# A four-layer conv kernel: layer 3 of the last image written out by hand in halves of its positions

## The chip, the cores and the metric

The kernel runs on one core of a Trainium2 chip. The metric is device time in microseconds for one launch. The kernel before took 2767.3 us (median of three runs, 2765.76 to 2767.45).

## What is computed

Two images of 512 channels and 32x32 positions go through four layers in f32: a deformable attention block with an MLP (layer 0), a global self-attention (layer 1), a position attention (layer 2) and a non-local block with squeeze-and-excitation (layer 3). The change touches the end: the results of layer 2 and all of layer 3, for the second image. Layer 3 is, per image:

```python
x_avg = jnp.mean(x, axis=(2, 3), keepdims=True)
se_mid = jax.nn.relu(conv1x1(x_avg, se1_w, se1_b))
W_cw = jax.nn.sigmoid(conv1x1(se_mid, se2_w, se2_b))
g_x = conv1x1(x, g_w, g_b).reshape(b, N)
theta_x = conv1x1(x, theta_w, theta_b).reshape(b, N)
phi_x = conv1x1(x, phi_w, phi_b).reshape(b, N)
f = theta_x[:, :, None] * phi_x[:, None, :]
f_div_C = jax.nn.softmax(f, axis=-1)
y = jnp.einsum('bij,bj->bi', f_div_C, g_x)
W_y = conv1x1(y, W_w, W_b)            # y has one channel
...
return W_cw * W_y + x                  # W_y after a batch norm with given statistics
```

So theta, phi and g are one number per position. For each of 1024 positions a softmax over 1024 others is taken of theta times phi, and g is averaged with it. The result y, one number per position, is scaled and shifted per channel and added to x.

## The kernel before

The image lies with channels on partitions: x2 is 128 x 4 x 2048 (four blocks of channels, two images of 1024 positions). Layers 0 and 1 come first and fill most of the time. Then image 0 goes through layer 2; after it, image 0's layer 3 is interleaved with image 1's layer 2 (`part(t)` is called between image 1's `l2_h` and `l2_attn` steps), and image 1's layer 3 comes last with nothing to interleave.

The functions that matter here:

- `l2_attn` (line 1416): 8 blocks of 128 positions of layer 2's attention. It exponentiates scores straight from PSUM (line 1435).
- `l2_out` (line 1445): z for both halves of 512 positions (`pz`, line 1450, eight accumulated matmuls each; copied by ScalarE, line 1457), then for each half and each block of channels a matmul `pr` (line 1461) and a VectorE instruction that adds it to x in place and sums x for the average (line 1469). `pr` has two PSUM buffers.
- `l3_scores` (line 1473): the rows theta, phi and g by four matmuls per half with 32 output partitions each (`prow`, line 1482), one two-bank PSUM tile for both halves, copied to SBUF (`rows3`, line 1489, ScalarE for half 0 and VectorE for half 1). A matmul with a broadcast selector spreads phi and then g over all partitions (`pp3`, line 1497), ScalarE copies each half to SBUF with its bias (`pg`, line 1504), VectorE takes the maximum and minimum of phi (lines 1508 and 1509). Transposes (line 1513) bring theta to one column per block of 128 positions (`th`, lines 1514 and 1517). `nm` (lines 1520 to 1524) is what is subtracted in the exponent.
- `part(t)` (line 1528): for one block of 128 positions ScalarE computes the exponential of 128x1024 with its sum (line 1530) and VectorE multiplies by g and sums (line 1538). `nd` collects numerators and denominators; `e3` has three buffers.
- `l3_out` (line 1544): y for all eight blocks (lines 1546, 1547), the squeeze-and-excitation weights `cw` (lines 1551 to 1568), `aff` with a scale and a shift per channel (line 1570), y broadcast to all partitions by eight matmuls (`py`, line 1575), and four results of 128x1024: block 0 by VectorE then ScalarE (1586, 1587), the others by ScalarE then VectorE (1589, 1590), each stored by the SP queue (1591), 512 KB each.

Order: outside of layer 0's hand-made part, a scheduler of the framework places the instructions on each engine; an instruction wrapped in `tc.keep_in_program_order` keeps its place in the order of the source on its engine. Each engine works its queue in order. Of this end, GpSimd (POOL) does nothing before the change: its last instruction is a memset of layer 1 (line 1289). The SP queue issues the stores.

## Time and profile before

| what | before |
|---|---|
| median of 3 runs | 2767.3 us |
| the profiled execution's own time | 2764.49 us |
| its span | 2762.7 us |
| TensorE busy | 2707.0 us (98%) |
| VectorE, ScalarE, GpSimd busy | 82%, 56%, 24% |
| granted TensorE clock, mean of the span | 0.996 |
| from the end of image 1's z matmuls to the end | 2718.25 to 2762.7 us |
| in 2735 to 2763 us: PE, DVE, ACT busy | 5.28, 15.66, 15.00 us of 28.00 |
| stores at the end (4 of 512 KB): issue to landing | 2.8 us (median) |

The profile is of one execution. PE is TensorE, DVE VectorE, ACT ScalarE, POOL GpSimd, SP the queue that issues the stores. L1538 is line 1538 of the kernel before. A group's line gives engine, operation, tiles written and read, shapes, count, then busy time and the mean of one, then idle time of the engine ahead of it and who ended it. The chain of waits is followed back from the last instruction; its lines are start, length and what ran. "issue" in it is time in which the profile shows no work and no wait. Matmuls in f32 appear as two passes, so one of 128x512 counts twice.

### The profile page before, as it was taken

The numbers are of one execution on the slowest core, as the hardware profiler recorded it, in microseconds if no ns is written. First come the engines' busy times: TensorE is split into PE (matmuls) and PEld (weight loads), VectorE is DVE, ScalarE is ACT, GpSimd is POOL, SyncE is SP. The second block draws the span as 40 slices with busy tenths as digits, with TensorE's granted clock in tenths as the row PEclk, the third lists the DMA queues.
The fourth block names the chain that finished last, engine by engine and source line by source line (L and its number), as shares of the span: only waits on it lengthen the run. The fifth ranks groups of instructions, "written<-read, shape, count | busy, mean of one in ns | idle before, by whom it ended". The sixth has DMA issues, their size and how long they took to land.

```text
span 2762.7 us, 49727 instructions
## 1 busy us (share of the span) xinstructions
PE 2707.0 (98%) x19782; PEld 987.5 (36%) x19782; DVE 2266.7 (82%) x2473; ACT 1544.3 (56%) x1950; POOL 663.6 (24%) x776
## 2 busy tenths in 40 slices
PE   8999999999999999999999999999999999999996
PEld 4233323233332323333333333333344444455543
DVE  6999999999999999999999999999654545523555
ACT  6676677667667776766776676676321111001244
POOL 0333333333333333333333333333100000000000
PEclk9999999999999999999999999999999999999998
DMA  3777777777777777777787778777400000100001
GB/s 121 160 163 155 161 154 160 158 160 158 154 164 149 162 163 158 161 161 156 167 185 172 152 165 193 154 170 159 102 30 23 16 23 23 70 7 0 0 1 61
DMA packets 145479, 335.14 MB, mean 121 GB/s; under 512 B 22592, under 2 KB 32064, under 8 KB 144480
## 3 DMA queue, kind: packets, MB, share of 16 engines
q0 software_dynamic: 77824, 201.38, 41.1%
q1 hardware_dynamic: 66992, 130.08, 13.2%
q8 instruction: 156, 2.56, 0.4%
q14 instruction: 75, 0.61, 0.1%
q10 hardware_dynamic: 432, 0.51, 0.1%
HBM read 58.99 MB, written 4.46 MB: 23 GB/s over the span
## 4 chain that ended last, share of the span: by engine, by line
PE 93%; ACT 3%; DVE 2%; issue 1%; DMA 1%; ACTq 0%; DVEq 0%; POOL 0%; SPq 0%; POOLq 0%
PE ph L616 61%; PE A L1101 4%; PE D L1101 4%; PE C L1101 4%; PE psim L669 2%; PE pr L1348 2%; PE B L1101 2%; PE po L1036 2%; PE pg L1244 1%; PE psim L654 1%; PE pz L1450 1%; PE pa L1339 1%; PE pu L1278 1%; ACT r L625 1%; PE pscore L1421 1%
## 5 line engine op out<-in xcount | busy, mean ns | idle before, releaser
L616 PE MATMUL ph<-h,w2a 128*32 128x512 f32 x16384 | 1790.7, 593 | 7.0 <-ACT r L625 6.9
L625 ACT ACTIVATE r<-ph,sb 128x1024 f32<-128x1024 f32 x1024 | 1141.4, 1115 | 562.3 <-PE ph L616 541.1
L349 DVE CUSTOM_DVE_ANT_1 h<-tab 128x1024 f32<-128x1024 f32 x1024 | 1205.9, 1220 | 8.6 <-PE ph L616 4.7
L616 PEld LDWEIGHTS ph<-h,w2a 128*32 128x32 f32 x16384 | 533.5, 109 | 1217.5 <-issue 833.1
L631 DVE SCALAR_TENSOR_TENSOR r<-r,rel,r 128x1024 f32<-128x1024 f32 x512 | 656.0, 1281 | 28.0 <-ACT r L625 27.3
L646 POOL DMA_DIRECT2D xs<-r x512 | 476.9, 1144 | 196.0 <-PE ph L616 95.7
L634 POOL DMA_DIRECT2D r<-r x256 | 222.2, 868 | 1107.2 <-DVE r L631 931.1
L172 ACT ACTIVATE tab<-tab,vec 128x256 f32<-128x256 f32 x252 | 137.1, 544 | 0.0
L1289 POOL MEMSET M<- 128x512 f32 x2 | 1.0, 520 | 439.6 <-DVE x L1165 439.6
L1141 ACT COPY u<-A 128x512 f32<-128x512 f32 x16 | 9.4, 585 | 146.9 <-PE A L1101 146.9
L1120 ACT ACTIVATE h<-h,vec 128x512 f32<-128x512 f32 x32 | 23.1, 721 | 113.6 <-DVE h L1123 113.6
L669 PE MATMUL psim<-xs,cw 128*32 128x512 f32 x512 | 72.1, 592 | 2.1 <-DMA xs<-r 2.1
L1123 DVE TENSOR_TENSOR h<-C,u 128x512 f32<-128x512 f32 x32 | 22.1, 691 | 48.8 <-PE C L1101 48.5
L1101 PE MATMUL A<-xn,w 128*128 128x512 f32 x128 | 60.2, 593 | 0.8 <-DVE x L1043 0.8
L1101 PE MATMUL C<-hT,w 128*128 128x512 f32 x128 | 60.3, 592 | 0.0
L1101 PE MATMUL A<-h,w 128*128 128x512 f32 x128 | 60.1, 592 | 0.0
L1036 PE MATMUL po<-q,vwo 128*128 128x512 f32 x128 | 56.4, 594 | 0.0
L1348 PE MATMUL pr<-x,A 128*128 128x512 f32 x128 | 55.1, 592 | 0.0
L229 DVE SCALAR_TENSOR_TENSOR acc<-q,vec,acc 128x128 f32<-128x128 f32 (+3 forms) x88 | 46.2, 525 | 0.8
L1161 DVE TENSOR_TENSOR x<-D,x 128x512 f32<-128x512 f32 x32 | 22.1, 691 | 26.0 <-PE D L1101 26.0
L852 ACT ACTIVATE e<-e,den 128x64 f32<-128x64 f32 x128 | 41.7, 336 | 2.7 <-DVE den L848 2.7
L1161 DVE TENSOR_TENSOR x<-C,x 128x512 f32<-128x512 f32 x32 | 22.1, 690 | 24.8 <-PE C L1101 24.8
(288 smaller groups left out, 1770.3 us busy)
## 6 DMA issues: line engine op xcount, KB each, us to landing
r<-r POOLq DMA_DIRECT2D x256, 512.0 KB, 4.7
xs<-r SPq DMA_DIRECT2D x512, 128.0 KB, 2.4
xs<-r POOLq DMA_DIRECT2D x512, 128.0 KB, 4.8
tab<-fd SPq DMA_DIRECT2D x63, 512.0 KB, 6.0
lw<-in_l_w_dram SPq DMA_DIRECT2D x5, 1024.0 KB, 10.2
x<-in_x_dram SPq DMA_DIRECT2D x4, 1024.0 KB, 8.5
w<-in_mlp_w_dram SPq DMA_DIRECT2D x8, 512.0 KB, 4.2
w<-in_mlp_w_dram SPq DMA_DIRECT2D x16, 256.0 KB, 3.2
```

The costliest lines, as they stand in the source:

```text
L172: return nc.scalar.activation(tf, tf if src is None else src[:, :, :, ax, :], AF.Identity, bias=0.0 if ax == 0 else v("L0_conv_cpb_b1"), s ...
L229: pin(nc.vector.scalar_tensor_tensor(dst, src, wt_, dst, ALU.mult, ALU.add))
L349: nc.vector._custom_dve(TENSOR_ADD_SAT, out=h1[:, h], in0=tab[:, j, h, 0, :].unsqueeze(1).to_broadcast([P, 32, 32]), in1=tab[:, j, h, 1, : ...
L616: nc.tensor.matmul(ph[t * 32 : (t + 1) * 32, i, :], lhsT=w2a[:, o], rhs=h1s[2 * p + i][:, h, half * 512 : (half + 1) * 512], start=True, s ...
L625: pin(nc.scalar.activation(r, ph, AF.Relu, bias=sb3[:, o, 1:2]))
L631: pin(nc.vector.scalar_tensor_tensor(r0, r1, rel[:, i : i + 1], r0, ALU.mult, ALU.add))
L634: pin(nc.gpsimd.dma_start(rs[p, 0], rs.pop((p, 2)), accum_op=ALU.add))
L646: pin(nc.gpsimd.dma_start(rs[p][i::2], r[i::2, i, :], accum_op=ALU.add))
L669: nc.tensor.matmul(psims[g, kb][m * 32 : (m + 1) * 32, :], lhsT=cw3[:, 3 - i : 35 - i], rhs=rs.pop(p + m), start=False, stop=(i == 3), ski ...
L1036: nc.tensor.matmul(po, lhsT=vwo[:, k * B + t // 2, o * P : (o + 1) * P], rhs=q[:, k, ts_], start=(k == 0), stop=(k == KC - 1),)
L1101: nc.tensor.matmul(banks[bank], lhsT=a[an][k], rhs=b_[bn_][k], start=(i < 4 and k == 0), stop=(k == n - 1), skip_group_check=True,)
L1348: nc.tensor.matmul(pr, lhsT=A[b][:, k, o * P : (o + 1) * P], rhs=x[:, k, ns], start=(k == 0), stop=(k == KC - 1),)
```

## The change

The second image's layer 2 results and layer 3 move into one new function, `last`, in which every instruction is wrapped in `keep_in_program_order`. In it:

- the work is cut into two halves of 512 positions; rows of half 0 are computed between results of layer 2, those of half 1 after them; each half has its own one-bank PSUM tile;
- theta's, phi's and g's biases are added when the rows are copied to SBUF (`b3`), phi and g stay in PSUM (two tiles of two banks from layer 2's score pool), the exponentials and the weighted sums read them there, the four copies to SBUF (`pg`) are gone;
- the squeeze-and-excitation weights are computed between the first weighted sums;
- y is formed and broadcast by halves, after the fourth and after the eighth weighted sum; results of the first half stand between the later weighted sums;
- results are 128x512: for blocks 0 to 2, POOL first adds the shift to x in place (`raised`), and VectorE then scales y and adds (`final`); for block 3, ScalarE scales and shifts y and POOL adds x (`final_act`);
- eight stores of 256 KB take the place of four of 512 KB, in the order of the source on the SP queue.

The built program has, besides, a library reload on POOL ahead of its first addition, and waits by which ScalarE's and VectorE's reads of one tile of y follow each other in the source's order (`final_act(3, 0)` after `final(1, 0)`, `final(2, 0)` after `final_act(3, 0)`, `final(0, 1)` after `final_act(3, 1)`).

```diff
@@ -1590,6 +1590,208 @@
                 nc.vector.tensor_tensor(r, r, xs, ALU.add)
             nc.sync.dma_start(out[b, o * P : (o + 1) * P].rearrange("c h w -> c (h w)"), r)
 
+    def last(b, fp, gp, fps, ps, gps, at2, ht):
+        pin = tc.keep_in_program_order
+        ve, pe, act = nc.vector, nc.tensor, nc.scalar
+        b3 = gp.tile([P, 1], F32, name="b3")
+        for i, name in enumerate(("theta", "phi", "g")):
+            first_ = i == 0
+            pin(
+                ve.tensor_tensor(b3, ident[:, i : i + 1], v(f"L3_conv_{name}_b"), ALU.mult)
+                if first_
+                else ve.scalar_tensor_tensor(b3, ident[:, i : i + 1], v(f"L3_conv_{name}_b"), b3, ALU.mult, ALU.add)
+            )
+        z = fp.tile([P, HW], F32, name="z")
+        rows3 = gp.tile([P, 2, 512], F32, name="rows3")
+        th = gp.tile([P, 8], F32, name="th")
+        ext = gp.tile([P, 2, 2], F32, name="ext")
+        top = gp.tile([P, 2], F32, name="top")
+        nm = gp.tile([P, 2, 8], F32, name="nm3")
+        nd = gp.tile([P, 2, 8], F32, name="nd")
+        y = gp.tile([P, 8], F32, name="y")
+        prow, pt = {}, {}
+        def at(o, half):
+            return x[:, o, b * HW + half * 512 : b * HW + (half + 1) * 512]
+        def out_z(half):
+            pz = ps.tile([P, 512], F32, name="pz", tag="ps")
+            for t in range(8):
+                rhs = at2[:, t, half * 512 : (half + 1) * 512]
+                pin(pe.matmul(pz, lhsT=ht[:, t, :], rhs=rhs, start=(t == 0), stop=(t == 7)))
+            pin(act.copy(z[:, half * 512 : (half + 1) * 512], pz))
+        def out_x(half, o):
+            pr = ps.tile([P, 512], F32, name="pr2", tag="ps")
+            zs = z[:, half * 512 : (half + 1) * 512]
+            pin(pe.matmul(pr, lhsT=l2wv[:, o * P : (o + 1) * P], rhs=zs, start=True, stop=True))
+            xs = at(o, half)
+            pin(
+                ve.scalar_tensor_tensor(
+                    xs, pr, v("L2_conv_bv", o), xs, ALU.add, ALU.add, accum_out=xavg[:, o, b, half : half + 1]
+                )
+            )
+        def row(half, k):
+            if k == 0:
+                prow[half] = gps.tile([P, 512], F32, name=f"prow{half}", tag="l3")
+            pin(
+                pe.matmul(
+                    prow[half][k * 32 : (k + 1) * 32, :], lhsT=w3x[:, k, :], rhs=at(k, half), start=True, stop=True
+                )
+            )
+            if k == KC - 1:
+                pin(act.activation(rows3[:, half, :], prow[half], AF.Identity, bias=b3))
+        pp = [fps.tile([P, 2, 512], F32, name="pscore") for _ in range(2)]
+        def spread(half, i):
+            to_all = c("sel3")[:, i : i + 1].to_broadcast([P, P])
+            pin(pe.matmul(pp[i][:, half, :], lhsT=to_all, rhs=rows3[:, half, :], start=True, stop=True))
+        def turn(half):
+            pt[half] = gps.tile([P, 4, P], F32, name=f"ptl{half}", tag="l3")
+            for t in range(4):
+                pin(pe.transpose(pt[half][:, t, :], rows3[:, half, t * P : (t + 1) * P], ident))
+        def theta(half):
+            rows_ = pt[half].rearrange("p t (k r) -> p t k r", k=KC)[:, :, :, 0]
+            pin(ve.tensor_reduce(th[:, half * 4 : half * 4 + 4], rows_, AX.X, ALU.add))
+        def extremes(half):
+            pin(ve.tensor_reduce(ext[:, 0, half : half + 1], pp[0][:, half, :], AX.X, ALU.max))
+            pin(ve.tensor_reduce(ext[:, 1, half : half + 1], pp[0][:, half, :], AX.X, ALU.min, negate=True))
+        def exponential(t):
+            e3 = es[t] = gp.tile([P, HW], F32, name="e3", bufs=3)
+            pin(
+                act.activation(
+                    e3,
+                    pp[0].rearrange("p a n -> p (a n)"),
+                    AF.Exp,
+                    bias=nm[:, 0, t : t + 1],
+                    scale=th[:, t : t + 1],
+                    accum_out=nd[:, 1, t : t + 1],
+                )
+            )
+        def weighted(t):
+            e3 = es.pop(t)
+            g3 = pp[1].rearrange("p a n -> p (a n)")
+            pin(ve.scalar_tensor_tensor(e3, e3, 1.0, g3, ALU.mult, ALU.mult, accum_out=nd[:, 0, t : t + 1]))
+        def mean(half):
+            hs = slice(half * 4, half * 4 + 4)
+            pin(ve.reciprocal(y[:, hs], nd[:, 1, hs]))
+            pin(ve.tensor_tensor(y[:, hs], y[:, hs], nd[:, 0, hs], ALU.mult))
+            py[half] = ps.tile([P, 512], F32, name="pyl", tag="ps")
+            for t in range(4):
+                to_all = y[:, half * 4 + t : half * 4 + t + 1].to_broadcast([P, P])
+                pin(pe.matmul(py[half][:, t * P : (t + 1) * P], lhsT=to_all, rhs=ident, start=True, stop=True))
+        def store(o, half, r):
+            pin(
+                nc.sync.dma_start(
+                    out[b, o * P : (o + 1) * P].rearrange("c h w -> c (h w)")[:, half * 512 : (half + 1) * 512], r
+                )
+            )
+        def raised(o, half):
+            xs = at(o, half)
+            pin(nc.gpsimd.tensor_tensor(xs, xs, aff[:, 1, o : o + 1].to_broadcast([P, 512]), ALU.add))
+        def final(o, half):
+            r = gp.tile([P, 512], F32, name="rl", bufs=6)
+            pin(ve.scalar_tensor_tensor(r, py[half], aff[:, 0, o : o + 1], at(o, half), ALU.mult, ALU.add))
+            store(o, half, r)
+        def final_act(o, half):
+            r = gp.tile([P, 512], F32, name="rl", bufs=6)
+            pin(act.activation(r, py[half], AF.Identity, bias=aff[:, 1, o : o + 1], scale=aff[:, 0, o : o + 1]))
+            pin(nc.gpsimd.tensor_tensor(r, r, at(o, half), ALU.add))
+            store(o, half, r)
+        es, py = {}, {}
+        out_z(0)
+        out_z(1)
+        for o in range(KC):
+            out_x(0, o)
+        out_x(1, 0)
+        out_x(1, 1)
+        for k in range(KC):
+            row(0, k)
+        out_x(1, 2)
+        out_x(1, 3)
+        for i in range(2):
+            spread(0, i)
+        for k in range(KC):
+            row(1, k)
+        turn(0)
+        extremes(0)
+        theta(0)
+        spread(1, 0)
+        turn(1)
+        spread(1, 1)
+        extremes(1)
+        theta(1)
+        pin(ve.tensor_reduce(top, ext, AX.X, ALU.max))
+        pin(ve.tensor_scalar(nm[:, 1, :], th, top[:, 0:1], -1.0, ALU.mult, ALU.mult))
+        pin(ve.scalar_tensor_tensor(nm[:, 0, :], th, top[:, 1:2], nm[:, 1, :], ALU.mult, ALU.min))
+        exponential(0)
+        avg = gp.tile([P, KC], F32, name="avg")
+        pin(ve.tensor_tensor(avg, xavg[:, :, b, 0], xavg[:, :, b, 1], ALU.add))
+        pin(ve.tensor_scalar(avg, avg, 1.0 / HW, None, ALU.mult))
+        pse = gps.tile([P, 2, 256], F32, name="psel", tag="l3")
+        for k in range(KC):
+            pin(
+                pe.matmul(
+                    pse[0:SE, 0, 0:1], lhsT=se1w[:, k, :], rhs=avg[:, k : k + 1], start=(k == 0), stop=(k == KC - 1)
+                )
+            )
+        mid = gp.tile([SE, 1], F32, name="mid")
+        pin(act.activation(mid, pse[0:SE, 0, 0:1], AF.Relu, bias=v("L3_conv_se1_b")[0:SE]))
+        for o in range(KC):
+            pin(pe.matmul(pse[:, 1, o : o + 1], lhsT=se2w[:, o * P : (o + 1) * P], rhs=mid, start=True, stop=True))
+        weighted(0)
+        cw = gp.tile([P, KC], F32, name="cw")
+        pin(ve.tensor_tensor(cw, pse[:, 1, 0:KC], v("L3_conv_se2_b"), ALU.add))
+        exponential(1)
+        exponential(2)
+        pin(act.activation(cw, cw, AF.Exp, scale=-1.0))
+        weighted(1)
+        weighted(2)
+        pin(ve.tensor_scalar(cw, cw, 1.0, None, ALU.add))
+        pin(ve.reciprocal(cw, cw))
+        aff = gp.tile([P, 2, KC], F32, name="aff")
+        pin(ve.tensor_tensor(aff, l3s, cw.unsqueeze(1).to_broadcast([P, 2, KC]), ALU.mult))
+        for half in range(2):
+            for o in range(3):
+                raised(o, half)
+        exponential(3)
+        weighted(3)
+        mean(0)
+        for t in range(4, 8):
+            exponential(t)
+        weighted(4)
+        weighted(5)
+        final(0, 0)
+        weighted(6)
+        final(1, 0)
+        final_act(3, 0)
+        weighted(7)
+        mean(1)
+        final(2, 0)
+        final_act(3, 1)
+        for o in range(3):
+            final(o, 1)
     with tc.tile_pool(name="f", bufs=2) as fp, tc.tile_pool(name="g", bufs=1) as gp:
         with tc.tile_pool(name="fps", bufs=2, space=PSUM) as fps:
             with tc.tile_pool(name="fp1", bufs=3, space=PSUM) as ps, tc.tile_pool(
@@ -1599,24 +1801,19 @@
                 ht = fp.tile([P, 8, MID], F32, name="ht")
                 at2 = l2_attn(0, fp, fps, ps, fg, lambda t: l2_h(0, t, ht, psh, "h"))
                 l2_out(0, fp, ps, at2, ht)
-            with tc.tile_pool(name="fp2", bufs=2, space=PSUM) as ps, tc.tile_pool(
-                name="gps", bufs=1, space=PSUM
-            ) as gps:
-                nd, part = l3_scores(0, gp, gps)
-                fg = l2_fg(1, fp, ps)
-                ht = fp.tile([P, 8, MID], F32, name="ht")
-                for t in range(8):
-                    l2_h(1, t, ht, ps, "ps")
-                    if t % 2:
-                        part(t // 2)
-                at2 = l2_attn(1, fp, fps, ps, fg, lambda t: part(4 + t // 2) if t % 2 else None)
-                l3_out(0, gp, gps, nd)
-                l2_out(1, fp, ps, at2, ht)
-        with tc.tile_pool(name="gpe", bufs=4, space=PSUM) as gps:
-            nd, part = l3_scores(1, gp, gps)
-            for t in range(8):
-                part(t)
-            l3_out(1, gp, gps, nd)
+            with tc.tile_pool(name="fp2", bufs=2, space=PSUM) as ps:
+                with tc.tile_pool(name="gps", bufs=1, space=PSUM) as gps:
+                    nd, part = l3_scores(0, gp, gps)
+                    fg = l2_fg(1, fp, ps)
+                    ht = fp.tile([P, 8, MID], F32, name="ht")
+                    for t in range(8):
+                        l2_h(1, t, ht, ps, "ps")
+                        if t % 2:
+                            part(t // 2)
+                    at2 = l2_attn(1, fp, fps, ps, fg, lambda t: part(4 + t // 2) if t % 2 else None)
+                    l3_out(0, gp, gps, nd)
+                with tc.tile_pool(name="gpl", bufs=2, space=PSUM) as gps:
+                    last(1, fp, gp, fps, ps, gps, at2, ht)
 
 
 def _layout(a):
```

## Prediction

> **What bounds the kernel now.** I read the page's table of 40 slices first: TensorE is the bound nearly everywhere (98% of the span), and only in the last slice does its digit fall from 9 to 6. So the whole change plays in the last 2%. Then I took the chain of waits from the end of image 0's results to the end:
>
> ```profile
> 2704.51 13.74 PE pz L1450 x32
> 2718.25 7.75 PE pr L1461 x16
> ...
> 2732.71 0.70 ACT pg L1504
> ...
> 2735.48 1.33 ACT e L1530 x2
> 2736.81 0.58 ACT pg L1504
> 2737.39 0.02 issue
> 2737.41 9.80 DVE e L1538 x16
> ...
> 2747.68 3.77 PE py L1575 x16
> 2751.45 0.03 issue
> 2751.47 1.29 DVE r L1586
> ```
>
> The columns are start, length and what was on the chain. TensorE leads until 2726, then a serial tail of 36.7 us follows in which each step waits for the one before: scores, eight weighted sums on VectorE, a broadcast of y, results, stores. To price the steps I took the groups of the last 68 us, kept apart by shape (count | busy, mean ns of one | idle before):
>
> ```profile
> L1530 ACT ACTIVATE e<-pg,nm,th 128x1024 f32<-128x1024 f32 x8 | 9.8, 1230 | 1.0 <-DVE nm L1524 1.0
> L1538 DVE SCALAR_TENSOR_TENSOR e<-e,pg 128x1024 f32<-128x1024 f32 x8 | 9.8, 1225 | 0.6 <-ACT pg L1504 0.6
> L1469 DVE SCALAR_TENSOR_TENSOR x<-pr,vec,x 128x512 f32<-128x512 f32 x8 | 6.0, 751 | 9.1 <-PE pr L1461 9.1
> L1435 ACT ACTIVATE e<-pscore,nm 128x1024 f32<-128x1024 f32 x3 | 3.4, 1129 | 0.0
> ```
>
> Last, the tail cut into microseconds (busy time of PE, PEld, DVE, ACT, POOL, then granted clock, DMA share, GB/s):
>
> ```profile
> 2750.00:2751.00 1.00, 1.00 (x6) 1.00 (x6) 0.00 (x0) 0.00 (x0) 0.00 (x0) 0.50 0.00 0
> ...
> 2759.00:2760.00 1.00, 0.00 (x0) 0.00 (x0) 0.00 (x0) 0.00 (x0) 0.00 (x0) 0.50 1.02 406
> 2760.00:2761.00 1.00, 0.00 (x0) 0.00 (x0) 0.00 (x0) 0.00 (x0) 0.00 (x0) 0.50 1.00 401
> ```
>
> The broadcast of y runs at half clock because TensorE sat idle for 11 us before it; the stores fill the DMA engines at 406 GB/s up to 2761.0; the program ends 1.7 us after the last byte, at 2762.7.
>
> **The sum, stage by stage.** Up to 2718.1 (end of pz) the built order of both kernels is the same on every engine, but for three 128x1 VectorE instructions (b3) that fall where VectorE is idle until 2719.1, and a library instruction on POOL, which has been idle since 2407. Times are on the clock of the profiled execution (2762.7 span, 2764.5 time; the median 2767.3 is 2.8 above that, so I apply the gain to the median).
>
> *To the first exponential.* Six results of layer 2 keep their pace (0.98 us each, two PSUM buffers; VectorE starts 2719.1 to 2724.0). Then TensorE inserts four row matmuls (1.07), which pushes the last two results from 2725.1 and 2726.0 to 2726.0 and 2726.9. But the first half's rows are in SBUF by 2725.8 (0.69 on ScalarE) and its two spreads run 2726.7 to 2728.4 instead of waiting; rows of half 1 end at 2729.4, the eviction 2730.2, spread 2730.4 to 2731.3. The extremes now read PSUM directly; a max and a min take 0.60 and 0.68 as L1508 and L1509 do: 2731.5 to 2732.7. Theta and three small instructions (0.1 to 0.2 each) give the first exponential at 2733.4, against 2735.5. Of that, the pg evictions (0.70 each on the path) are the main part. **-2.1.**
>
> *Weighted sums.* Exponentials from PSUM: the nearest row, L1435, has the same shape and source, 1.13 against L1530's 1.23. That saves nothing more: VectorE sets the pace. VectorE's g now comes from PSUM. L1469 and L1586 with a PSUM operand are 0.06 longer than the multiply-add without one, but they also have a pointer operand; the additions from PSUM without one (128x512, 691 ns) are in step with 1220 ns for 1024 from SBUF (0.53 us for 512 elements more). I take no extra cost (bounds 0 to 0.06, 0.5 in all). First weighted sum 2734.7. Eight at 1.225 = 9.8; between them stand the cw addition, which waits for se2 (0.2), cw+1, its reciprocal and aff, each dependent (0.5), mean(0), 0.35, and two results of 128x512 at 0.70 (1.4). So the last ends at 2746.9, against 2747.2. From the first exponential that is 13.5 us instead of 11.7: **+1.8.** Hidden under it: y's first broadcast (1.9 at half clock, 2740.7 to 2742.6, first asked for at 2743.1), the squeeze-excite matmuls and POOL's six additions.
>
> *y and its broadcast.* mean(1) is 0.35 instead of 0.46; four broadcasts instead of eight at half clock, 1.9 instead of 3.75 (TensorE will have idled 5 us, so I keep half clock; at full clock 1.0). **-2.0.** A VectorE result (final(2, 0), 0.7) lies under it.
>
> *Results.* Before: from 2751.5 to 2758.6, four results of 1024 in a ScalarE-VectorE chain, 7.1. After 2749.2: ScalarE forms final_act(3, 1) (0.74), POOL adds x (1.2, see below), store at 2751.2. VectorE's last three results wait for ScalarE's read of the same y (a wait in the built program), then take 2.1, to 2752.1. The SP queue holds their stores behind final_act's store, in that order. **-5.1** for the first of these stores.
>
> *Stores.* Before, last store issued 2758.6, end 4.1 later. After, four of 256 KB are queued within 1 us of 2751.2: 0.78 to the first byte (2756.3 to 2757.1 in the trace), 1.05 MB at 406 GB/s = 2.6, and the same 1.7: 5.1. VectorE's last at 2752.1 fits in: its data could start at 2753.0, its turn comes at 2753.9. **+1.0.**
>
> Sum: -2.1 + 1.8 - 2.0 - 5.1 + 1.0 = -6.4 (end near 2756.3).
>
> **POOL, the unknown.** No POOL addition is in the trace: POOL's only compute rows are memsets (128x512: 520 ns, which read nothing); VectorE's addition of that size is 691. The Trainium skill's "GPSIMD Engine Reference" (section "Performance versus the Vector engine") speaks against the change: it calls GpSimd about half as fast on two-input elementwise work, 4497 ns for 2048 elements. By the row an addition costs 0.7, by the page 1.1 to 1.35; I take 1.2 as an estimate. Six start at 2739.4 (aff) and end at 2746.6, each before its reader (first 2740.6 for 2743.1; fourth 2744.2 for 2750.0), and final_act(3, 0)'s at 2747.8. Only the last addition is on the path; by VectorE's row the end would be 0.5 earlier.
>
> The second rule: "SBUF — State Buffer", section "Who interferes with whom", says that a VectorE instruction with two SBUF inputs is locked out while a GpSimd instruction reads SBUF, and the other way round. The weighted sums and results read PSUM and one SBUF operand, so they escape; y times nd in mean(0) (128x4, 0.17 in the trace) does not. At 2740.5 it meets POOL's additions. By the row it costs nothing more; by the rule up to one addition, 1.2. No run here shows it; I take the middle, **+0.6**, as VectorE is the bound there. mean(1) at 2747.1 can meet the seventh addition, which also moves.
>
> Total -5.8: end 2756.9, time 2767.3 - 5.8 = 2761.5.
>
> **Rivals.**
> 1. *POOL is starved or starving.* If POOL's queue keeps the lock through all six additions, mean(0) waits until 2746.6, weighted(4) starts 6 us late, the end is about 2762.2 and the time 2766.8: no change. For it: six additions stand back to back in one queue. Against: a waiting VectorE instruction should get in between two. Chance 0.08.
> 2. *POOL's additions become the bound: slower.* All eight stand in one queue from 2739.4, so the end is 2739.4 + 8d + 5.1, with d the price of one. Up to d = 1.5 only the last counts; at 2.3 the whole gain is gone; at 3.0 the end is 2768.5, time 2773, slower. Against: the page's 1.1 to 1.35, half of the turning point. For: no row here. Chance 0.06.
> 3. *POOL's first addition pays for loading its code.* The built program has a library reload ahead of it. POOL reaches it at 2407, and then the load is hidden by 330 us of idleness; if it comes at first use instead, 6 us (that page, section "Instruction dispatch"), the first result waits to 2746.6, the last addition ends near 2755 and the end is 2760.0: gain 2.7, 2764.6. Chance 0.10.
> 4. *Better than thought:* no lock, the last broadcast at full clock: gain 7.3, 2760.0. Chance 0.08.
> That the change does not do what it says is excluded by the built order, which has these instructions as written.
>
> **How the numbers follow.** The forecast (0.68) spans gains of 5.2 (lock 1.2) to 6.4 (none), with perhaps 0.5 of missed latencies. What a measurement tells from no change is about 0.2%, or 5.5 us, which lies inside the forecast; I give 0.45 of its 0.68 to beyond that bound and 0.23 to within. Faster by over 0.2%: 0.45 + 0.08 = 0.53. Within: 0.23 + rivals 1 and 3, 0.18, + 0.01 of rival 2 = 0.42. Slower: 0.05. The range 2759.7 to 2765.5 holds the forecast, rival 4 and rival 3, and leaves out rivals 1 and 2. The forecast's own range is 2760.5 to 2762.6.
>
> **What would show it.** The first exponential near 2733.4, 2 us earlier than L1530; weighted sums at 1.23; y's multiplication in mean(0) 0.2 long or up to 1.3; POOL's additions starting 1.2 apart; four broadcasts in 1.9; the DMA full for 2.6 us at the end. Wrong if VectorE's gaps between weighted sums 3 and 4 exceed 2 us, if POOL's seventh addition ends after 2750, or if the last stores start later than 2752.5.

## The result, and the profile after

The changed kernel takes 2761.15 us (median of 16 runs, 2757.97 to 2762.80) against 2766.01 for the kernel before in the same session (16 runs, 2765.57 to 2768.11): 4.9 us less, a ratio of 0.998 with a 95% interval of 0.9973 to 0.9987. The forecast was 5.8 less. The profiled execution took 2762.35 us with a span of 2760.6, at a mean granted clock of 0.995 (before 0.996).

The two spans differ by only 2.1 us, because the unchanged part of the after trace lies 3.2 us later (the last section shows half of it). So all that follows is counted from the start of the first `pr` matmul, a point with the same work ahead of it in every kernel here. From there to the end, which I call the tail, it is 44.58 us before and 39.25 after.

The chain of waits of the changed kernel, from the second half's rows to the end (start, length, what was on the chain):

```profile
2733.01 0.70 ACT rows L1646
...
2733.75 1.14 PE pscore L1653 x2
...
2736.96 1.29 ACT e L1671 x2
...
2746.54 0.71 DVE rl L1710
2747.26 1.14 DVE e L1684 x2
2748.39 0.66 DVE rl L1710
2749.05 1.14 DVE e L1684 x2
2750.19 0.10 DVE y L1689
2750.29 0.02 issue
2750.32 0.98 DVE y L1690
2751.30 0.04 issue
2751.34 2.09 PE pyl L1694 x8
2753.43 0.03 issue
2753.45 0.79 ACT rl L1715
```

The copies to SBUF (`pg`, 0.70 and 0.58 on the old chain) are gone. But two results (`rl`) now stand on the chain between weighted sums, and y's multiplication, 128x4 elements, takes 0.98. The broadcast is 2.09 instead of 3.77. Behind it only one ScalarE step (0.79) and one POOL addition (1.27) stand ahead of the first of the last four stores, where a chain of four results stood before the last store.

The groups of the last part by shape (count | busy, mean ns of one | idle before) answer to L1530, L1538 and L1469 of before:

```profile
L1684 DVE SCALAR_TENSOR_TENSOR e<-e,pscore 128x1024 f32<-128x1024 f32 x8 | 9.6, 1214 | 1.1 <-ACT e L1671 1.1
L1671 ACT ACTIVATE e<-pscore,nm,th 128x1024 f32<-128x1024 f32 x8 | 9.5, 1185 | 3.3 <-DVE nm L1745 3.3
...
L1706 POOL TENSOR_TENSOR x<-x,aff 128x512 f32<-128x512 f32 x6 | 6.0, 1030 | 332.9 <-DVE aff L1773 332.9
L1632 DVE SCALAR_TENSOR_TENSOR x<-pr,vec,x 128x512 f32<-128x512 f32 x8 | 6.0, 751 | 9.4 <-PE pr L1629 9.3
...
L1716 POOL TENSOR_TENSOR rl<-rl,x 128x512 f32<-128x512 f32 x2 | 2.5, 1264 | 3.9 <-ACT rl L1715 3.9
```

POOL's additions cost 1.03 each with a broadcast second operand and 1.26 with two whole tiles. The exponentials fell from 1230 to 1185 ns. The weighted sums' own length hardly fell (1225 to 1214), but their pace did: in the chain each takes 1.14 of the path.

The tail's last microseconds (busy time of PE, PEld, DVE, ACT, POOL, granted clock, DMA share, GB/s):

```profile
2751.00:2752.00 1.00, 0.66 (x3) 0.66 (x4) 0.95 (x2) 0.00 (x0) 0.27 (x1) 0.50 0.00 0
...
2757.00:2758.00 1.00, 0.00 (x0) 0.00 (x0) 0.00 (x0) 0.00 (x0) 0.00 (x0) 0.50 1.04 383
2758.00:2759.00 1.00, 0.00 (x0) 0.00 (x0) 0.00 (x0) 0.00 (x0) 0.00 (x0) 0.50 1.01 379
```

The broadcast still runs at half clock, and the DMA engines are full for under 3 us, at 383 GB/s with rows of 2 KB where before it was 406 with rows of 4 KB.

By stage, in us from the tail's start:

| stage | before | after | change | forecast |
|---|---|---|---|---|
| to the first exponential | 17.39 | 15.63 | -1.76 | -2.1 |
| from there to the end of the last weighted sum | 11.74 | 13.23 | +1.49 | +1.8, and +0.6 for a lock |
| y and its (last) broadcast | 4.22 | 3.23 | -0.99 | -2.0 |
| to the issue of the deciding store (before the last, after the first of four) | 7.15 | 2.19 | -4.96 | -5.1 |
| from there to the end | 4.08 | 4.97 | +0.89 | +1.0 |
| sum | 44.58 | 39.25 | -5.33 | -5.8 |

My theory after this table: the gain comes from what stands behind the last y (smaller results, an early half, y by halves); the results between the weighted sums and POOL's additions bring nothing or cost. The rival: the interleaving and POOL are what let the last stores go early, and without them the end would be later.

### The profile page after: what moved, and what is told of

It is laid out like the page before. It is cut to its first block, busy times and chain, and to the rows that moved or that the text cites. A ratio compares the mean times of both kernels' runs of the same rounds, so it can differ in the third digit from the quotient of the medians.

```text
span 2760.6 us, 49753 instructions
## 1 busy us (share of the span) xinstructions
PE 2710.6 (98%) x19782; PEld 989.0 (36%) x19782; DVE 2266.0 (82%) x2477; ACT 1540.0 (56%) x1945; POOL 671.0 (24%) x784
## 4 chain that ended last, share of the span: by engine, by line
PE 93%; ACT 3%; DVE 2%; issue 1%; DMA 1%; DVEq 0%; ACTq 0%; POOL 0%; SPq 0%; POOLq 0%
PE ph L616 61%; PE A L1101 4%; PE D L1101 4%; PE C L1101 4%; PE psim L669 2%; PE pr L1348 2%; PE B L1101 2%; PE po L1036 2%; PE pg L1244 1%; PE psim L654 1%; PE pa L1339 1%; PE pu L1278 1%; ACT r L625 1%; PE pscore L1421 1%; PE pz L1623 0%
## 5 line engine op out<-in xcount | busy, mean ns | idle before, releaser
L1706 POOL TENSOR_TENSOR x<-x,aff 128x512 f32<-128x512 f32 x6 | 6.0, 1030 | 332.9 <-DVE aff L1773 332.9
```

## The experiments

The ratios are each kernel's own against runs of the kernel before on its chip, with 95% intervals. Every tail is that of the kernel's profiled execution; the change run a second time (the last experiment) shows how far one can be trusted.

One step moves the tails from execution to execution. In the ten profiles of changed kernels without unread matmuls, the granted clock falls to half between 17.2 and 20.2 us after the tail's start. The four `se2` matmuls run from about 17.1 (18.3 with the copies back), and where the clock falls before they end, `cw` and with it the second weighted sum come later. First the change, then the kernel without POOL, which has the same work up to there:

```profile
2738.44 1.35 PE L1761 MATMUL psel<-mid,se2w 32*128 32x1 f32 x8 [0.71 <-ACT mid L1759]
```

```profile
2736.88 1.05 PE L1761 MATMUL psel<-mid,se2w 32*128 32x1 f32 x8 [0.71 <-ACT mid L1759]
```

So a table at the end of this section also counts from the start of the second weighted sum.

**The results of the first half, last.** All of them behind mean(1):

```diff
         weighted(4)
         weighted(5)
-        final(0, 0)
         weighted(6)
-        final(1, 0)
-        final_act(3, 0)
         weighted(7)
         mean(1)
+        final(0, 0)
+        final(1, 0)
+        final_act(3, 0)
         final(2, 0)
...
```

> The changed kernel with one thing undone: the results of the first half (final(0,0), final(1,0), final_act(3,0)) no longer stand between the weighted sums; all results come after mean(1). I compare the tail, from the end of the last z matmul to the end of the span: 44.5 us before, 39.1 in the changed kernel. Theory (VectorE is the bound between the weighted sums, and TensorE's second broadcast covers about 2 us of VectorE work): the two results of 0.70 leave the stretch ahead of y (-1.4), POOL's addition no longer meets y's multiplication (-0.8), but now five VectorE and ScalarE results stand behind mean(1) with only 2.1 us of cover, and all eight stores leave together, 2.1 MB at 383 GB/s = 5.5 us instead of 2.8. Net +0.5 to +2, tail 39.6 to 41. Rival (the interleaving is what brings the gain): tail at least 42.5, most of the 5.3 us lost.

Measured: tail 37.97, median 2760.05, ratio 0.9975 [0.9966, 0.9984]. It is 1.3 shorter than the change. The last weighted sum ends at 27.69 instead of 28.86, y's multiplication takes 0.24 instead of 0.97, and the last broadcast ends at 30.19 instead of 32.09: 1.9 gained there, 0.73 of it because POOL's addition for block 3 no longer meets the multiplication. 0.6 is given back behind it, where eight stores now leave between 28.75 and 34.28. I had charged the stores more than that: this expectation was too high. The interleaving costs 1.3, the meeting included; it brings nothing on balance.

**phi and g copied to SBUF again**, and read there:

```diff
...
+        def copied(half, i):
+            pin(act.activation(pg[:, i, half, :], pp[i][:, half, :], AF.Identity))
...
-                    pp[0].rearrange("p a n -> p (a n)"),
+                    pg[:, 0].rearrange("p a n -> p (a n)"),
...
-            g3 = pp[1].rearrange("p a n -> p (a n)")
+            g3 = pg[:, 1].rearrange("p a n -> p (a n)")
...
```

> The changed kernel with one thing undone: ScalarE copies phi and g from PSUM to SBUF again, the extremes, exponentials and weighted sums read the copies; halves, order, POOL and stores as in the changed kernel. Theory: the copy stands ahead of the last extremes (+0.7), the copy of g's second half stands ahead of the first weighted sum (+0.6), and eight weighted sums go from 1.14 to 1.225 start to start (+0.7): tail 39.1 + 2.0 = 41.1. Rival (reading PSUM from two engines at once costs as much as it saves): tail within 0.5 of 39.1.

Measured: tail 42.58, median 2764.08, ratio 0.9992 [0.9983, 1.0]. The loss is 3.3, where I had expected 2.0. Two lines of its groups, and four of its timeline (start, length, instruction), show the rest:

```profile
L1689 DVE SCALAR_TENSOR_TENSOR e<-e,pg 128x1024 f32<-128x1024 f32 x8 | 10.8, 1364 | 1.7 <-ACT pg L1658 1.7
L1711 POOL TENSOR_TENSOR x<-x,aff 128x512 f32<-128x512 f32 x6 | 10.7, 1815 | 334.7 <-ACT e L1676 334.7
```

```profile
2744.07 7.73 POOL L1711 TENSOR_TENSOR x<-x,aff 128x512 f32<-128x512 f32 x4 [334.74 <-ACT e L1676]
...
2745.02 0.78 DVE L1695 TENSOR_TENSOR y<-y,nd 128x4 f32<-128x4 f32 x1
...
2746.87 2.05 DVE L1689 SCALAR_TENSOR_TENSOR e<-e,pg 128x1024 f32<-128x1024 f32 x1
...
2748.85 0.74 DVE L1715 SCALAR_TENSOR_TENSOR rl<-pyl,aff,x 128x512 f32<-128x512 f32 x1
```

With both tiles in SBUF a weighted sum takes up to 2.05 and POOL's additions 1815 ns instead of 1030: they hold each other up. The result L1715, which has one of its tiles in PSUM, stays at 0.74 in the same stretch. This is the rule of the Trainium skill's "SBUF — State Buffer", "Who interferes with whom" (two SBUF inputs on VectorE against a GpSimd instruction that reads SBUF), now with this case's numbers.

**The meeting at mean(1) avoided**, first attempt: `final_act(3, 0)` moved behind mean(1) in the source.

```diff
-        final_act(3, 0)
         weighted(7)
         mean(1)
+        final_act(3, 0)
         final(2, 0)
```

> The changed kernel with final_act(3, 0) moved behind mean(1), so that POOL's seventh addition cannot run while VectorE multiplies y by nd there (in the changed kernel that multiplication took 0.97 us, in mean(0) 0.16). Theory (VectorE is locked out by a POOL addition that reads two whole tiles): the multiplication takes 0.16 and the tail is 0.8 shorter, 38.3. Rival (the long multiplication waits for something else, such as nd's last accumulator or a pipeline flush): it stays at 0.97, tail 39.1.

Measured: tail 38.95, median 2761.12, ratio 0.9981 [0.9973, 0.9988]. It tells nothing of the meeting, since the edit did not remove it: the order of the source binds only each engine's own queue. ScalarE had nothing else to do and ran the step at 27.54, POOL added at 28.39 to 29.66, and y's multiplication still took 0.97.

**The same, second attempt**: x is added to block 3's first half by VectorE, behind mean(1).

```diff
-        final_act(3, 0)
...
+        pin(act.activation(r3, py[0], AF.Identity, bias=aff[:, 1, 3:4], scale=aff[:, 0, 3:4]))
         weighted(7)
         mean(1)
+        pin(ve.tensor_tensor(r3, r3, at(3, 0), ALU.add))
+        store(3, 0, r3)
```

> The changed kernel with one addition moved from POOL to VectorE: block 3 of the first half is scaled by ScalarE as before, but VectorE adds x, behind mean(1), under the second broadcast. (Moving final_act in the source had left POOL's addition where it was, since ScalarE had nothing else to do.) Theory (VectorE's multiplication of y was locked out by POOL's addition): it takes 0.16 to 0.24 instead of 0.97 and the tail is 0.8 shorter than 39.2, near 38.4. Rival: the 0.97 stays, 39.2.

Measured: tail 38.89, median 2760.94, ratio 0.9979 [0.9971, 0.9988]. Two lines of the changed kernel's timeline, then the same step here:

```profile
2750.01 1.26 POOL L1716 TENSOR_TENSOR rl<-rl,x 128x512 f32<-128x512 f32 x1 [0.84 <-ACT rl L1715]
...
2750.32 0.97 DVE L1690 TENSOR_TENSOR y<-y,nd 128x4 f32<-128x4 f32 x1
```

```profile
2748.91 0.16 DVE L1690 TENSOR_TENSOR y<-y,nd 128x4 f32<-128x4 f32 x1
```

In the change the multiplication ends (2751.29) when POOL's addition ends (2751.27). Without that addition it takes 0.16. From the end of the last weighted sum to the end of the program it is 9.59 here against 10.39 in both executions of the change: 0.80, the lock's price. Of that the tail shows only 0.36, since in this execution `cw` came 0.4 later (second weighted sum at 19.10 against 18.66).

**POOL left out.** ScalarE scales and shifts all eight results, VectorE adds x:

```diff
-        for half in range(2):
-            for o in range(3):
-                raised(o, half)
...
+        def scaled(o, half):
+            r = rs[o, half] = gp.tile([P, 512], F32, name="rl", bufs=6)
+            pin(act.activation(r, py[half], AF.Identity, bias=aff[:, 1, o : o + 1], scale=aff[:, 0, o : o + 1]))
+        def added(o, half):
+            r = rs[o, half]
+            pin(ve.tensor_tensor(r, r, at(o, half), ALU.add))
...
-        final(0, 0)
         weighted(6)
-        final(1, 0)
-        final_act(3, 0)
+        added(0, 0)
         weighted(7)
         mean(1)
...
```

> The changed kernel without POOL: ScalarE forms scale times y plus shift from PSUM for all four blocks of both halves, VectorE adds x (128x512 each), stores in the order of blocks; the first half's addition of block 0 stands between the last two weighted sums, the other three under the second broadcast. Theory (POOL's work is hidden, only its last addition and the lock are on the path): one VectorE result fewer ahead of y (-0.7), no lock (-0.8), first store 0.78 + 0.7 after the broadcast instead of 0.78 + 1.3 (-0.6), but four in a ScalarE chain of 0.72 each, so the last store leaves 3.7 after the broadcast and its data follow 0.8 later: -0.2 to -0.6 for the end in all against the store-bound tail. Tail 37 to 38. Rival (POOL's help is what makes the results cheap): four results behind the broadcast cost more than before the change per element, tail 40 or more.

Measured: tail 36.91, median 2758.49, ratio 0.9972 [0.9961, 0.9982]. It is 2.3 shorter than the change (2.7 by the medians), with one first-half result before the last weighted sum and no lock (both multiplications 0.16). POOL as a helper is not needed: ScalarE was free. Stage by stage, the 2.3 are 0.3 ahead of the second weighted sum (the clock), 0.6 up to the end of the last one (one result fewer between the sums), 0.8 at y's multiplication (no lock) and 0.6 behind the last broadcast (7.16 to 6.53).

**POOL's work doubled**: behind each of the six additions a second one into a scratch tile that nobody reads.

```diff
             pin(nc.gpsimd.tensor_tensor(xs, xs, aff[:, 1, o : o + 1].to_broadcast([P, 512]), ALU.add))
...
+            pin(nc.gpsimd.tensor_tensor(again, xs, aff[:, 1, o : o + 1].to_broadcast([P, 512]), ALU.add))
```

> The changed kernel with each of POOL's six shift additions followed by a second one of the same form into a scratch tile that nothing reads: POOL's queue is 12 additions long instead of 6 ahead of the two for block 3. It tells two rivals apart. If y's multiplication is let in between two POOL additions, it takes at most 1.2 us in both means, although POOL's queue is full around each of them; if the queue keeps the lock (rival), the multiplication in mean(0) waits 5 us or more. And the price of POOL as the bound: 12 additions at 1.03 end 34.2 us after the tail's start (21.8 + 12.4), the two for block 3 at 36.7 instead of 34.3, their stores and those behind them in the SP queue follow: tail 39.2 + 2.4 = 41.7. If POOL is not on the path at all, 39.2.

Measured: tail 42.39, median 2764.46, ratio 0.9992 [0.9984, 1.0001]. Its timeline around mean(1):

```profile
2749.03 1.04 POOL L1706 TENSOR_TENSOR x<-x,aff 128x512 f32<-128x512 f32 x1
...
2749.87 0.22 DVE L1690 TENSOR_TENSOR y<-y,nd 128x4 f32<-128x4 f32 x1
...
2750.15 1.04 POOL L1708 TENSOR_TENSOR again<-x,aff 128x512 f32<-128x512 f32 x1
```

POOL's queue is full here, yet the multiplication ends at 2750.09, with the addition that was running (2750.07), and POOL's next one starts after it. Between these two additions there is a gap of 0.08, but so there is between the other pairs. The kernel with the copies back has none there (POOL's first addition ends at 25.28 and the next starts at 25.25), and the multiplication in mean(0) ends with the first one, at 25.29. A full POOL queue does not keep the lock; it costs at most the rest of one addition. The loss of 3.1 comes from POOL's own last additions, which start at 34.76 and 35.98.

**TensorE kept busy** by eleven f32 matmuls of 128x512 whose result nobody reads (1 before the average, 5 before the first weighted sum, 5 behind mean(0)):

```diff
+        def warm(n):
...
+            for _ in range(n):
+                pin(pe.matmul(pd, lhsT=ident, rhs=rows3[:, 0, :], start=True, stop=True))
```

> The changed kernel with eleven f32 matmuls of 128x512 that nothing reads put into TensorE's idle stretches: one ahead of the squeeze-excite matmuls, five between them and the first broadcast of y, five between the two broadcasts. Theory (half clock after idling doubles the second broadcast, which lies on the path): the broadcast takes 1.05 instead of 2.08 us and the tail is 1.0 shorter, 38.2. Rival (the five matmuls still run at half clock, 1.7 us each, and stand in the way of y's broadcasts): the second broadcast starts 2 to 4 us late, tail 41 to 43.

Measured: tail 38.51, median 2759.5, ratio 0.9977 [0.9968, 0.9985]. The second broadcast in this kernel's timeline:

```profile
2748.18 1.16 PE L1694 MATMUL pyl<-cst,y 128*128 128x128 f32 x8 [0.66 <-DVE y L1690]
```

The granted clock in that microsecond is 1.00, and the four broadcasts take 1.16 where the change takes 2.08. Half clock on the last broadcast costs about 0.9, and it is to be had back. The tail is only 0.74 shorter, as the matmuls also stood in the way: y's first half was ready at 22.63, its broadcast began at 24.19, and the seventh weighted sum, with the first result ahead of it, began 2.34 after the sixth instead of 1.85. Against that, `cw` came 0.3 earlier.

**No POOL, results behind mean(1), and the same eleven matmuls.**

> A version that the runs so far point to: no POOL (as in the run without it, tail 36.9), all four results of the first half behind mean(1), and the matmuls that keep TensorE's clock. Theory: one result of 0.65 less ahead of y, broadcast 1.05 instead of 2.08; then VectorE is the bound from mean(1) on, with eight additions at 0.66 = 5.3 us from 27.6, so the last store leaves at 32.9 instead of 33.95: tail 35.8. Rival (matmuls in the way): 38 or more.

Measured: tail 36.92, median 2759.01, ratio 0.9972 [0.9962, 0.9982]. A miss. Without the lock y was ready at 27.46, but the broadcast began only at 29.34: the five matmuls behind mean(0) stood in TensorE's queue, as this kernel's timeline shows (y's multiplication ended at 2748.36).

```profile
2745.95 4.46 PE L1751 MATMUL pd<-rows,cst 128*128 128x512 f32 x10
...
2750.25 1.05 PE L1694 MATMUL pyl<-cst,y 128*128 128x128 f32 x8
```

The matmuls that keep the clock have to be sized to the gap that they fill.

**The same with six matmuls** (1, 3 and 2):

```diff
-        warm(5)
+        warm(3)
...
-        warm(5)
+        warm(2)
```

> The version without POOL and with all first-half results behind mean(1), with six unread matmuls instead of eleven: one ahead of squeeze-excite, three and two in the two gaps, so that they end before y is ready (in the run with eleven, the second broadcast began 1.8 us after y, since the five before it ran until 29.3). Theory: second broadcast from 27.5 to 28.6 us after the tail's start, VectorE adds eight results from 27.4 on, ScalarE's chain for the second half starts at 28.6, last store near 32.5; eight stores of 256 KB from 28.1 on then bound the end: tail 35.6. Rival (half clock stays half with so little work): broadcast 2.1, tail 36.3 or more, as in the run without POOL (36.9).

Measured: tail 35.80, median 2758.37 (2755.82 to 2759.76), ratio 0.9969 [0.9958, 0.9981]. The end of its timeline on the path:

```profile
2748.18 0.16 DVE L1690 TENSOR_TENSOR y<-y,nd 128x4 f32<-128x4 f32 x1
2748.27 5.04 DVE L1716 TENSOR_TENSOR rl<-rl,x 128x512 f32<-128x512 f32 x8
...
2748.40 1.16 PE L1694 MATMUL pyl<-cst,y 128*128 128x128 f32 x8 [1.97 <-DVE y L1690]
```

y follows the last weighted sum at once, the broadcast runs at full clock, and it runs beside VectorE's first additions. It has the shortest tail of all, 3.45 under the change and 1.1 under the kernel without POOL; the medians of these two (2758.37 and 2758.49) do not tell them apart. What binds its end now are the stores: the DMA engines are full from 2750 to 2755, at 371 to 387 GB/s.

**y in one piece**: the first variant (results last), with mean(0) moved to just before mean(1).

> The run with all results behind mean(1) (tail 38.0), with one thing more undone: y's first half, too, is formed and broadcast only after the last weighted sum. Theory (the gain of the results stage comes from y by halves: the first half's broadcast is hidden and its results lie under the second's): 4.2 us of broadcasts at half clock stand behind the last weighted sum, results of the first half start 2.2 later, those of the second half too: tail 38.0 + 2.2 to 2.5 = 40.3. Rival (the gain comes from the results' shape and their split over VectorE, ScalarE and POOL alone): tail 38.5 or less.

Measured: tail 39.81, median 2761.67, ratio 0.9983 [0.9976, 0.999]. The broadcasts then take 27.63 to 31.41 in a row. It is 1.84 longer than with mean(0) early. Its second weighted sum began 0.49 earlier, so counted from there the loss is 2.33, 0.3 of it a longer meeting with POOL (the first multiplication takes 0.52). So y by halves is worth about 2.

**Copies to SBUF without POOL** (the two edits together).

> The run without POOL (tail 36.9) with the copies of phi and g to SBUF put back, as in the run that put them back with POOL in place (which cost 3.3 us: weighted sums that read two SBUF tiles and POOL's additions held each other up, weighted sums up to 2.05 us and additions 2.02). Theory: with no POOL, copies cost only the chain to the first exponential (0.7), g's second copy ahead of the first weighted sum (0.5), and ScalarE's slower exponentials (1.225 against 1.18 start to start, four of them bound at most): +1.2 to +1.6, tail 38.1 to 38.5. Rival (SBUF reading itself is slow, not the meeting with POOL): +3, tail 40.

Measured: tail 38.76, median 2760.27, ratio 0.9978 [0.997, 0.9986]. It is 1.85 above the kernel without POOL, and all of that lies ahead of the second weighted sum (20.34 against 18.34). The first exponential waits 0.67 longer (16.29 against 15.62). The copy of g's second half stands ahead of `mid` on ScalarE, which puts the se2 matmuls another 0.5 later. They then run at half clock, 1.87 instead of 1.05. The copies themselves thus cost about 1.2; the other 0.8 is the clock, which in that execution of the kernel without POOL fell only after se2. With POOL at work the copies cost 3.3, of which 1.6 lies behind the second weighted sum: the meeting of VectorE and POOL. From SBUF the exponentials start 1.22 to 1.24 apart instead of 1.18, but weighted sums with nothing in between are still 1.14 apart (20.34, 21.48).

**The change once more.**

> The changed kernel once more, beside the others on one chip. Theory: the tail is 39.2 give or take 0.6, as its parts move only with where TensorE's clock steps fall; the time differs from run to run by more, since the stretch ahead of the tail shifts by up to 3 us.

Measured: tail 39.15, median 2761.15 (2758.09 to 2762.94), ratio 0.9981 [0.9974, 0.9988]. Two executions of one kernel differ by 0.1 in the tail (y's multiplication 0.97 in both), but the clock's fall can move a tail by up to 0.8, so small differences mean something only where a step is named for them. Counted from the start of the second weighted sum (us from the tail's start), the executions that do the same work agree to 0.01:

| kernel | second weighted sum starts | tail | from there to the end |
|---|---|---|---|
| the change | 18.66 | 39.25 | 20.59 |
| the change once more | 18.55 | 39.15 | 20.60 |
| final_act(3, 0) moved, first attempt | 18.36 | 38.95 | 20.59 |
| block 3 added by VectorE | 19.10 | 38.89 | 19.79 |
| first-half results last | 18.85 | 37.97 | 19.12 |
| the same, y in one piece | 18.36 | 39.81 | 21.45 |
| copies back | 20.38 | 42.58 | 22.20 |
| no POOL | 18.34 | 36.91 | 18.57 |
| no POOL, copies back | 20.34 | 38.76 | 18.42 |
| no POOL, results last, six matmuls | 18.33 | 35.80 | 17.47 |

## Why the prediction was right, and where its steps were off

The total (-5.8, measured -4.9 by the medians and -5.3 by the tails) and its main terms held. The results behind the last y were 5.1 and are 4.96; the first exponential was to come 2.1 earlier and came 1.76 earlier (the first half's two spreads took 1.88 instead of 1.7, the second half's rows stand behind them, and its first spread took 1.13 instead of 0.9); the stores were +1.0 and are +0.89.

Part of the fit is luck. Against the forecast the five stages are off by +0.3, -0.9, +1.0, +0.1 and -0.1 us, which comes to no more than +0.5. And the time, 2761.15, lies in the forecast's own range because the kernel before, too, was 1.3 faster in the runs beside the changed kernel (2766.01 against 2767.3); the gain of 4.9 by the medians is a little below the 5.2 to 6.4 that the forecast spanned. Of its signs of being wrong, two stayed away: from the start of the fourth weighted sum to that of the fifth it is 1.43, and POOL's seventh addition ends at 2748.0, on the clock of the trace before. The third came in part: the last four stores start at 2752.4 to 2753.8 on that clock, where 2752.5 was the bound.

One reading behind a term that held was wrong as well. The prediction put most of the earlier first exponential down to the copies. But only one copy, 0.70, stood on the path ahead of it, and with the copies put back it starts at 16.32, 0.69 later than in the change. The other 1.07 of the 1.76 goes with the order by halves. That order was not tried alone, but it fits two steps that are off the chain after, the last addition to x and the transposes:

```profile
2726.02 0.77 DVE x L1469 x2
...
2730.77 0.76 PE pt L1513 x7
```

What failed inside is three terms, of which the first offsets the other two in part.

1. "That saves nothing more: VectorE sets the pace." This was wrong, and the timeline of the kernel before has it:

```profile
2737.29 1.23 ACT L1530 ACTIVATE e<-pg,nm,th 128x1024 f32<-128x1024 f32 x1
...
2738.51 1.23 ACT L1530 ACTIVATE e<-pg,nm,th 128x1024 f32<-128x1024 f32 x1
...
2738.64 1.23 DVE L1538 SCALAR_TENSOR_TENSOR e<-e,pg 128x1024 f32<-128x1024 f32 x1
```

The exponential that began at 2737.29 ended at 2738.52, and 0.12 later the weighted sum that reads it began; so it went on, every 1.22 us, at ScalarE's pace. I had taken two equal durations for VectorE's own pace. Free of that wait, a weighted sum starts every 1.14 us, from PSUM and from SBUF alike (the latter in the kernel with copies and without POOL). Eight of them are 0.7 shorter than the 9.8 I summed. Together with the lock that mean(0) escaped, it is why this stage was +1.49 and not +2.4. Against it, `cw` held up the second weighted sum by 0.56 instead of 0.2, since the clock fell during the se2 matmuls (1.35 instead of 1.05).
2. The lock. I charged half of one POOL addition at mean(0). It came at mean(1), where I had written that it can meet and had given it no price: 0.80 there (block 3 added by VectorE). mean(0) escaped because its multiplication started only 0.08 before POOL's first addition ended, as the timeline of the change shows:

```profile
2743.15 6.02 POOL L1706 TENSOR_TENSOR x<-x,aff 128x512 f32<-128x512 f32 x6 [332.94 <-DVE aff L1773]
...
2744.10 0.16 DVE L1690 TENSOR_TENSOR y<-y,nd 128x4 f32<-128x4 f32 x1
```

This margin is narrow, but no accident of one execution: it is 0.08 or 0.09 in all seven profiles with this order, since POOL's first addition and the weighted sum ahead of mean(0) both follow `aff`. The prediction's own times (additions of 1.2 from 2739.4, the multiplication at 2740.5) already left only 0.1 us of an addition to wait for. The size was the rule's, up to one addition; the place was wrong.
3. The last broadcast at half clock is 2.08, not 1.9. With the lock this makes -0.99 out of -2.0.

The rivals: POOL starving VectorE is refuted (doubled work, and copies back: the lock ends with the running addition). POOL as the bound is far off in the change: an addition costs 1.00 to 1.26, where 2.3 would have taken the gain; only with its work doubled do POOL's last additions set the end, and then 3.1 of the 5.3 are lost. For that cost the Trainium skill's "GPSIMD Engine Reference" (section "Performance versus the Vector engine") was the better guide than VectorE's 0.69: a quarter of its 4497 ns for 2048 elements, as an estimate, is 1.12. A code load at the first addition did not appear: POOL's library instruction ran at 2410.2, 333 us ahead, and the first addition took 1.03. "Better than thought" needed full clock and no lock; the variant with six matmuls shows that both were to be had, though not by the change itself.

What the prediction did not ask is whether each part of the change earns its place. Of three parts that I tried alone, two do: reading PSUM instead of copying (about 1.2 without POOL, and 0.8 more where the clock falls ahead of se2; 3.3 with POOL) and y by halves (about 2). The third, the first half's results between weighted sums, costs 1.3: VectorE is the bound there and each of the two, 0.66, stands on the path, and the meeting with POOL adds 0.73. They were meant to relieve the stores; without them the stretch behind the last broadcast is only 0.6 longer. POOL's additions replace work that ScalarE can do in idle time, and without them it is 2.3 faster, of which the lock is 0.8 and one result fewer between the sums 0.6. Open stays how the 0.6 behind the last broadcast divides between POOL and the other order of the results, since that variant changes both. The smaller results and stores were not undone alone. They show only in the variant with y in one piece: from its last broadcast to the end it is 8.40, against 11.23 in the kernel before.

## What to carry to other kernels

In a serial tail, ask of each edit which engine ends last in that stage: work moved between the steps of the engine that bounds it is on the path, however short (0.66 each here). What paid was halving the work around a wait, so that one half runs while the other waits. A helper engine whose instructions hold up those of the bound engine has a price even if its own work is hidden (0.80 here). Keep one operand of the bound engine in PSUM if that avoids it, as it did here (a result stayed at 0.74), or leave the helper out. Before calling an engine the one that sets a pace, look at whether its start times follow its own ends or another engine's. And when two variants are compared by one execution each, count from behind the last step that moves by chance.

## What the runs showed of the hardware that was not expected

The place where POOL and VectorE met. A 128x4 multiplication took 0.97 instead of 0.16 beside an addition of 1.26, and in a full POOL queue only 0.22: what is paid is the rest of the addition that is running. All meetings of this kind in the traces fit that. With 0.96, 0.77, 0.50, 0.22 and 0.21 of an addition left, the multiplication took 0.97, 0.78, 0.52, 0.24 and 0.22; with 0.08 left it took its usual 0.16. The cost is thus set by timing, to within one addition.

Unread matmuls bring the broadcast from 2.08 to 1.16, the granted clock from 0.50 to 1.00; six of them placed well do it, and eleven can stand in the way.

The clock also moved far from the tail. At 1961 us, in layers that neither kernel changes, matmuls of `po` ran at half clock in the profiled execution of the change and at full clock in that of before. Before:

```profile
1961.00:1962.00 1.00, 1.00 (x3) 0.38 (x2) 0.00 (x0) 0.00 (x0) 0.00 (x0) 1.00 0.95 168
1962.00:1963.00 1.00, 1.00 (x4) 0.47 (x3) 0.32 (x1) 0.00 (x0) 0.00 (x0) 1.00 0.98 168
```

After:

```profile
1961.00:1962.00 1.00, 1.00 (x2) 0.45 (x2) 0.69 (x1) 0.00 (x0) 0.78 (x1) 0.50 1.11 213
1962.00:1963.00 1.00, 1.00 (x2) 0.34 (x1) 0.00 (x0) 0.00 (x0) 0.00 (x0) 0.50 1.03 184
```

The granted clock, before the DMA columns, is 1.00 and then 0.50. This cost about 1.5 of the 3.2 us by which the unchanged part lies later in that execution. In the other profiles that shift is between -0.1 and +2.8, so a single execution cannot show a change of 5 us in this kernel; the tails and the medians can.
